# First loads in smaller pieces, P1 and P2 in two PSUM banks, and the last product in three banks of a factorization-machine kernel

## The chip, the cores and the metric

The kernel runs on one core of a Trainium2 chip. The metric is the device time of one execution in microseconds (us), median of a few runs. A profile of one execution is shown beside it.

## The reference

All data is float32. `x` is 1024 x 512 (batch, feature), `weight` is 64 x 512 x 512 (embedding, feature, model), `lin_w` is 512 x 512, `lin_b` has 512 values.

```python
out_lin = x @ lin_w.T + lin_b
xv = jnp.einsum('bf,efm->bem', x, weight)
zp = jnp.einsum('bf,efm->bem', jnp.square(x), jnp.square(weight))
interaction = 0.5 * jnp.sum(jnp.square(xv) - zp, axis=1)
return out_lin + interaction
```

There are three parts: a linear layer, a large product `xv` whose squares are summed over the 64 embeddings, and `zp`, which after the sum over embeddings is one product of the squared `x` with the summed squares of the weights.

## The kernel before, in words

**Work and tiling.** Features are split as 128 partitions times four slices k. Every matrix product is cut into 2 x 2 blocks and done by a scheme of seven block products (P1 to P7) with sums of blocks ahead of them and behind them; for `xv` the scheme is applied twice, one inside the other. Three stretches follow each other on TensorE:

- the linear layer: seven products of blocks of `x` (A11, A12, A21, A22 and sums R3, R5, R6, R7 of them) and blocks of `lin_w` (and sums lt1 to lt4 of them). It is written through `lin_product`, which calls `big_product` (L397);
- `xv`: eight groups of seven trees with seven products each (`tree`, L558, matmuls at L580), the bulk of the time;
- `zp`: seven products again (`zp_product`, L768, also through `big_product`), whose results are added to the output with the linear part.

A `big_product` fills a PSUM tile of two banks, [128, 2, 512]: half u = 0 or 1 holds two batch tiles of 128 rows with 256 model columns each. One half is two batch tiles times two slices k, four matmuls in the code and, in the records, eight weight loads and eight matmul instructions of 128x256 (each float32 matmul shows as two). With `by_k=True` the product is cut into four steps (k, u), so that it can start on the first slices.

**First loads.** `x` comes in transposed (`xT`, feature by batch). SP's queue brings eight pieces of 256 KB into `oa0` to `oa3`, ScalarE's queue four pieces of 256 KB of `lin_w` into `ob0` and `ob1` (L323 to L331). A11 is `oa0` (x slices k = 0 and 1, first batch half), A12 is `oa1` (k = 2 and 3), A21 and A22 are `oa2` and `oa3`, the second batch half. `lin_w`'s blocks are `ob0` (k = 0, 1) and `ob1` (k = 2, 3), each with column halves c = 0 and 1. Rows of a transfer are 2 KB. After these, SP's queue brings the weights.

**Zero matmuls.** VectorE zeroes the tile `t4_1`, and TensorE multiplies it by itself twice, 512 columns wide, into the bank pair `b2_1`, which is later overwritten (L334 to L338).

**P1, P2 and what follows.** P1 = A11 x block (0,0) of `lin_w` goes to `b2_0`. ScalarE copies each half of P1 to `b2_1`, where P6 and P7 are added to it later. P2 = A12 x block (1,0) is accumulated on P1 in `b2_0`, and a ScalarE copy takes the sum to `ob2`, which is stored. P4 = A22 x lt4 goes to `b1`, P5 = R5 x lt1 to `b3`, and so on (L458 to L478). VectorE makes lt1 to lt4 in `column_sums` (L385): t1 = b[1] - b[0], t2 = b[3] - t1, t3 = b[3] - b[1], t4 = b[2] - t2. The products need these; R5 = A22 - A21 and the other sums come from `x_sum` (L357). ScalarE copies A11, A12 and A22 into `x_all` (L355).

**The end.** The last product, `zp` P4, goes to `b2_1`; `add_part` (L749) subtracts half of it from the output rows in `w22a`, in two halves of 512 columns per partition on VectorE, and each half is stored by a transfer of 256 KB.

**What sets the order.** `Plan` (L30) is a list scheduler that runs when the program is built. Each step has a cost on its engine, reads, writes, and, for TensorE, a key that fixes its place. `order` gives each engine its fixed sequence; a VectorE, ScalarE, GpSimd or SP step is taken by the latest time at which it may start. `landing` tells the planner when a load is expected. Semaphores between engines are added to the emitted order automatically, from the tiles that are read and written. So a planned time decides only the order; the chip decides when.

Of the kernel before, what the change touches and what calls it, by code (L numbers as in the profile page):

```python
# [12 lines left out]
AF = mybir.ActivationFunctionType  # L13
ALU = mybir.AluOpType
AX = mybir.AxisListType

P = 128
G = 2
# [8 lines left out]
PE, DVE, ACT, POOL, SP = "PE", "DVE", "ACT", "POOL", "SP"  # L27
# [156 lines left out]
def kernel(  # L184
# [34 lines left out]
    nc = tc.nc  # L219
    NG, NQ, _, NCB, KH, N = weight.shape  # L220
    B = xT.shape[1]
    M = out.shape[1]
    NB = B // P
# [4 lines left out]
    H = B // 2  # L228
    Q = B // 4
# [11 lines left out]
    buf = {}  # L241
# [35 lines left out]
    plan = Plan()  # L277
# [18 lines left out]
    def act(o, i, func, reads, writes, cost=1.04):  # L296
        def emit(_):
            if func is None:
                nc.scalar.copy(o, i)  # L299
            else:  # L300
                nc.scalar.activation(o, i, func)  # L301

        plan.add({ACT: cost}, emit, reads, writes)
# [10 lines left out]
    def dma(o, i, reads, writes, move=1.75):  # L314
        plan.add({SP: 0.45}, lambda _: nc.sync.dma_start(o, i), reads, writes, land=2.0, move=move)


    x_src = xT.rearrange("(p k) b -> p k b", k=NK)
    lw_src = lin_wT.rearrange("(p k) m -> p k m", k=NK)
    def landing(name, at):  # L320
        plan.add({SP: 0.0}, None, (), (name,), land=at)

    for h, order in enumerate(((0, 1, 2, 3), (2, 3, 0, 1))):  # L323
        for at, k in enumerate(order):
            q, r = divmod(k, KH)
            n, l = f"oa{2 * h + q}", f"ob{q}"
            nc.sync.dma_start(buf[n][:, r, :], x_src[:, k, ts(h, H)])
            landing((n, r), (4.4 + 1.6 * at, 10.2 + 0.9 * at)[h])
            if h == 0:
                nc.scalar.dma_start(buf[l][:, r, :], lw_src[:, k, :])  # L330
                landing((l, r), 4.4 + 1.6 * at)  # L331


    zero = buf["t4_1"]  # L334
    nc.vector.memset(zero, 0.0)  # L335
    for j in range(G):
        nc.tensor.matmul(buf["b2_1"][:, j, :], zero[:, 0:P], zero, start=True, stop=True)  # L337
    plan.add({PE: 4.0}, None, (), (("b2_1", 0), ("b2_1", 1)), key=-2000)  # L338

    def block4(i):  # L340
        return buf[f"X{i}"][:, 0:4, :].rearrange("p (k q) b -> p k (q b)", k=2)
# [2 lines left out]
    a_buf = {"A11": "oa0", "A12": "oa1", "A21": "oa2", "A22": "oa3"}  # L344

    def a_parts(*names):
        return tuple((a_buf[n], r) for n in names if n in a_buf for r in range(KH)) + tuple(
            n for n in names if n not in a_buf
        )

    def a_ap(n):
        return buf[a_buf[n]] if n in a_buf else block4(int(n[1]))

    for i, n in ((1, "A11"), (2, "A12"), (4, "A22")):
        act(block4(i), a_ap(n), None, a_parts(n), (f"R{i}",))  # L355
# [23 lines left out]
    HM = M // 2  # L379

    def quarter(ap):

        return ap.rearrange("p a (b m) -> p (a b) m", b=2)
# [13 lines left out]
    def big_product(bank, lhs, rhs, first, keys, by_k=False):  # L397

        (a, a_names), (b, b_names) = lhs, rhs
        steps = [(u, [k]) for k in range(KH) for u in range(G)]  # L400
        for (u, ks), key in zip(steps if by_k else [(u, range(KH)) for u in range(G)], keys):
            def emit(_, u=u, ks=ks):
                for j in range(2):
                    for k in ks:
                        nc.tensor.matmul(  # L405
                            buf[bank][:, u, ts(j, HM)],
                            a[:, k, ts(2 * u + j, P)],
                            b[:, k, :],
                            start=first and j == 0 and k == 0,
                            stop=k == KH - 1,  # L410
                            skip_group_check=True,
                        )

            names = sum((a_names[k:k + 1] + b_names[k:k + 1] for k in ks), ()) if by_k else (
                a_names + b_names
            )
            plan.add({PE: PAIR * len(ks) / KH}, emit, names + ((bank, u),), ((bank, u),), key=key)

    def both_halves(bank):
        return (bank, 0), (bank, 1)  # L420

    lw_quad = [buf[f"ob{q}"][:, :, ts(c, HM)] for q in range(2) for c in range(2)]
    lw_names = [tuple((f"ob{q}", r) for r in range(KH)) for q in range(2) for _ in range(2)]
    lt = {
        k: buf[("p5_2", "p53_2")[(k - 1) // 2]][:, (k - 1) % 2, :].rearrange(
            "p (k m) -> p k m", k=KH
# [1 line left out]
        for k in range(1, 5)  # L428
    }
    lt_names = {k: (("lt", k),) for k in range(1, 5)}  # L430
    column_sums(DVE, lw_quad, lt, lw_names, lt_names)
    lhs = {i: (a_ap(n), a_parts(n)) for i, n in (
        (1, "A11"), (2, "A12"), (4, "A22"), (5, "R5"), (6, "R6"), (7, "R7"), (3, "R3"))}
    rhs = {1: (lw_quad[0], lw_names[0]), 2: (lw_quad[2], lw_names[2]),
           3: (lw_quad[3], lw_names[3]), 4: (lt[4], lt_names[4]),
           5: (lt[1], lt_names[1]), 6: (lt[2], lt_names[2]), 7: (lt[3], lt_names[3])}

    def lin_product(p, bank, first, key, last=None, by_k=False):
        keys = [key, last or key + 0.2, key + 0.4, key + 0.6]
        big_product(bank, lhs[p], rhs[p], first, keys, by_k)  # L440

    def lin_store(n, h, c):
        dma(lin_dram[:, ts(h, NB // 2), ts(c, HM)], quarter(buf[n]), (n,), (("lind", h, c),))

    def lin_last(n, bank, sign):

        def emit(_):
            if sign > 0:
                nc.vector.tensor_add(buf[n], buf[bank], buf[n])
            else:  # L450
                nc.vector.scalar_tensor_tensor(
                    buf[n], buf[n], -1.0, buf[bank], ALU.mult, ALU.subtract
                )

        reads = both_halves(bank) if bank.startswith("b") else (bank,)
        plan.add({DVE: 1.14}, emit, (n, *reads), (n,))

    lin_product(1, "b2_0", True, -1000, by_k=True)  # L458
    for u in range(G):
        act(buf["b2_1"][:, u, :], buf["b2_0"][:, u, :], None, (("b2_0", u),), (("b2_1", u),), 0.56)  # L460
    lin_product(2, "b2_0", False, -999, by_k=True)
    act(buf["ob2"], buf["b2_0"], None, both_halves("b2_0"), ("ob2",))
    lin_store("ob2", 0, 0)
    lin_product(4, "b1", True, -998)
    act(buf["c_0"], buf["b1"], None, both_halves("b1"), ("c_0",))
    lin_product(5, "b3", True, -997)
    act(buf["c_1"], buf["b3"], None, both_halves("b3"), ("c_1",))
    lin_product(6, "b2_1", False, -996)
# [11 lines left out]
    for lo, hi in ((0, 1), (1, 7)):  # L480
        a11, a21, a12, a22, s1, s2, s4 = (x_all[:, lo:hi, s, :] for s in range(7))
        raw, names, done = (tuple(f"{c}{i + 1}" for i in range(lo, hi)) for c in "RXY")
# [8 lines left out]
    def used(*names):  # L491

        plan.add({SP: 0.0}, None, (), names, land=-plan.HOP)

    for n in tuple(a_buf.values()) + ("ob0", "ob1"):
        used(n, (n, 0), (n, 1))
    for b in ("b1", "b3", "b2_0", "b2_1"):
        used(b, *both_halves(b))
    used("p5_2", ("lt", 1), ("lt", 2))
# [157 lines left out]
    for g in range(NG):  # L657
# [6 lines left out]
        order = ORDER if g else ORDER_0  # L664
# [12 lines left out]
        if g + 1 < NG:  # L677
            names = tuple((acc_name[g], *k) for k in acc_parts)
# [18 lines left out]
    for h, c in blocks:  # L697
        n, rows = lin_all[h, c], ts(h, NB // 2)
# [10 lines left out]
    lhs = {p: (buf[xe[b]], (xe[b],)) for p, b in ((1, (0, 0)), (2, (0, 1)), (4, (1, 1)))}  # L709
    a21 = (buf[xe[1, 0]], (xe[1, 0],))  # L710
    for p, a, b, kind in (
# [6 lines left out]
        a, b = (lhs[z] if isinstance(z, int) else z for z in (a, b))  # L718
# [5 lines left out]
        for q in range(2) for c in range(2)  # L724
# [5 lines left out]
    rhs = {1: (w2_quad[0], w2_names[0]), 2: (w2_quad[2], w2_names[2]),  # L730
           3: (w2_quad[3], w2_names[3])}
# [13 lines left out]
    out_dst = out.rearrange("(n p) m -> p n m", p=P)  # L745
    last_key = 7 * (7 * NG - 1) + PLACE[4]
    bank_a, bank_2, bank_b, bank_3 = "b1", "b2_0", "b2_1", "b3"

    def add_part(h, c, bank, store, halves=False):  # L749

        n = lin_all[h, c]
        for u in range(G) if halves else (slice(None),):
            o, b = buf[n][:, u], buf[bank][:, u]
            name = (n, u) if halves else n
            plan.add(
                {DVE: 0.61 if halves else 1.14},
                lambda _, o=o, b=b: nc.vector.scalar_tensor_tensor(  # L757
                    o, b, -0.5, o, ALU.mult, ALU.add
                ),
                (((bank, u),) if halves else both_halves(bank)) + (n,), (name,),  # L760
            )
            if store:
                lo = NB // 2 * h + (2 * u if halves else 0)
                src = o.rearrange("p (b m) -> p b m", b=2) if halves else quarter(o)
                dma(out_dst[:, lo:lo + (2 if halves else 4), ts(c, HM)], src, (name,), (),
                    0.9 if halves else 1.75)

    def zp_product(p, bank, first, key):  # L768
        big_product(bank, lhs[p], rhs[p], first, [last_key + key, last_key + key + 0.2])
# [14 lines left out]
    zp_product(3, bank_3, False, 5)  # L784
    add_edge(0)
    add_part(0, 1, bank_3, True)
    zp_product(4, bank_b, True, 6)
    add_part(1, 0, bank_b, True, True)

    for op, engine in plan.order():  # L790
        if op.emit:
# [32 lines left out]
```

## Time and profile before

| | us |
|---|---|
| median of 3 runs | 1409.09 (1408.12 to 1409.17) |
| profiled execution | 1408.17 |
| its span, first to last instruction | 1406.4 |
| TensorE busy | 1398.7 |
| GpSimd busy | 1039.1 |
| VectorE busy | 1079.7 |
| ScalarE busy | 693.4 |

The span is the time from the first to the last instruction of the core; the time of the execution is a little longer. In the profile, PE is TensorE's matmuls, PEld its weight loads, DVE VectorE, ACT ScalarE, POOL GpSimd, SP SyncE, whose queue starts most transfers; "q" marks the sequencer or the queue of an engine. L12 is line 12 of the kernel. Groups of instructions carry the tile written and the tiles read (out<-in, without buffer numbers: `b` stands for `b1`, `b3`, `b2_0` and `b2_1`, and `p` for the buffers that hold lt1 to lt4 at the start). The mean granted TensorE clock in the record is 0.999 of full speed.

### The profile page before, as it was taken

How to read it: one execution, taken by the hardware profiler on the slowest of the kernel's cores; microseconds unless marked ns; L12 is line 12 of the kernel's file. 1: busy time of each engine (PE TensorE's matmuls, PEld its weight loads, DVE VectorE, ACT ScalarE, POOL GpSimd, SP SyncE). 2: the span in 40 equal slices, each digit the busy share in tenths (PEclk: the TensorE clock that was granted, in tenths of full speed). 3: DMA queues.
4: the chain of work that ended last, by engine and by line, in shares of the span. 5: the costliest groups of instructions: out<-in, count | busy, mean ns of one | idle time of the engine just before them, and what ended most of it. 6: DMA issues, size and time to landing. Idle time of an engine off the chain costs nothing.

```text
span 1406.4 us, 10559 instructions
## 1 busy us (share of the span) xinstructions
PE 1398.7 (99%) x3364; PEld 639.1 (45%) x3364; DVE 1079.7 (77%) x929; ACT 693.4 (49%) x721; POOL 1039.1 (74%) x706
## 2 busy tenths in 40 slices
PE   9999999999999999999999999999999999999998
PEld 6444444444444444444444444444444444444446
DVE  7977696867959687696867859687696867859676
ACT  3545363544636455463544636455463545636442
POOL 5686786958678686776958678596777958678694
PEclk9999999999999999999999999999999999999999
DMA  5673562917538183562917537283563907447355
GB/s 224 164 174 96 124 179 80 237 46 178 155 97 206 45 222 96 134 175 85 232 39 185 148 105 198 55 224 85 144 182 81 228 31 194 138 113 194 90 119 118
DMA packets 53863, 197.57 MB, mean 140 GB/s; under 512 B 19120, under 2 KB 29360, under 8 KB 31920
## 3 DMA queue, kind: packets, MB, share of 16 engines
q0 software_dynamic: 15312, 84.81, 31.4%
q1 hardware_dynamic: 37920, 111.03, 22.4%
q10 hardware_dynamic: 576, 1.05, 0.2%
q8 instruction: 28, 0.46, 0.1%
q14 instruction: 27, 0.22, 0.0%
HBM read 173.93 MB, written 6.16 MB: 128 GB/s over the span
## 4 chain that ended last, share of the span: by engine, by line
PE 99%; DVE 0%; ACT 0%; DVEq 0%; issue 0%; ACTq 0%
PE b L580 96%; PE b L405 4%; PE b L337 0%; ACT b L299 0%; DVE w22a L757 0%; DVEq L820 0%; DVE t L335 0%; ACTq L299 0%
## 5 line engine op out<-in xcount | busy, mean ns | idle before, releaser
L580 PE MATMUL b<-t,x_all 128*128 128x512 f32 x1792 | 805.9, 592 | 0.0
L580 PEld LDWEIGHTS b<-t,x_all 128*128 128x128 f32 x1792 | 340.4, 190 | 427.8 <-issue 422.4
L580 PE MATMUL b<-w,x_all 128*128 128x512 f32 x768 | 358.1, 592 | 0.0
L287 POOL TENSOR_TENSOR t<-w 128x512 f32<-128x512 f32 x128 | 177.1, 1384 | 155.4 <-PE b L580 86.5
L299 ACT COPY p<-b 128x1024 f32<-128x1024 f32 x161 | 161.9, 1006 | 165.4 <-PE b L580 165.4
L580 PEld LDWEIGHTS b<-w,x_all 128*128 128x128 f32 x768 | 145.9, 190 | 183.3 <-issue 172.9
L287 POOL TENSOR_TENSOR t<-w,t 128x512 f32<-128x512 f32 x128 | 177.1, 1384 | 62.7 <-PE b L580 62.7
L301 ACT ACTIVATE oa<-oa 128x1024 f32<-128x1024 f32 x124 | 129.7, 1057 | 139.0 <-DVE oa L287 136.1
L580 PE MATMUL b<-T,x_all 128*128 128x512 f32 x384 | 180.4, 592 | 0.0
L308 DVE TENSOR_REDUCE acc<-oa 128x16 f32<-128x1024 f32 x124 | 149.0, 1211 | 38.7 <-ACT oa L301 38.7
L299 ACT COPY b<-b 128x1024 f32<-128x1024 f32 (+1 forms) x116 | 114.2, 985 | 125.1 <-PE b L580 120.8
L308 DVE TENSOR_REDUCE w_sum<-wsq 128x16 f32<-128x1024 f32 x128 | 154.7, 1210 | 19.4 <-ACT wsq L301 19.4
L287 DVE TENSOR_TENSOR oa<-b,p 128x1024 f32<-128x1024 f32 x95 | 115.9, 1220 | 41.0 <-PE b L580 40.8
L287 POOL TENSOR_TENSOR t<-T 128x512 f32<-128x512 f32 x64 | 90.3, 1411 | 57.8 <-issue 33.2
L301 ACT ACTIVATE wsq<-w 128x1024 f32<-128x1024 f32 x96 | 97.9, 1056 | 66.0 <-DVE w_sum L308 66.0
L301 ACT ACTIVATE c<-c 128x1024 f32<-128x1024 f32 x68 | 70.1, 1056 | 92.4 <-POOL c L287 63.0
L580 PEld LDWEIGHTS b<-T,x_all 128*128 128x128 f32 x384 | 73.0, 190 | 91.8 <-issue 91.4
L287 DVE TENSOR_TENSOR ob<-b,p 128x1024 f32<-128x1024 f32 x48 | 58.6, 1221 | 67.3 <-PE b L580 67.3
L287 DVE TENSOR_TENSOR p<-b,p 128x1024 f32<-128x1024 f32 x79 | 96.3, 1219 | 17.5 <-PE b L580 17.4
L287 POOL TENSOR_TENSOR t<-T,t 128x512 f32<-128x512 f32 x64 | 81.3, 1270 | 20.5 <-PE b L580 20.5
L287 POOL TENSOR_TENSOR ob<-ob,p 128x1024 f32<-128x1024 f32 x32 | 91.9, 2884 | 0.0
L287 POOL TENSOR_TENSOR c<-oa,p 128x1024 f32<-128x1024 f32 x32 | 90.7, 2834 | 0.0
(86 smaller groups left out, 1408.6 us busy)
## 6 DMA issues: line engine op xcount, KB each, us to landing
w<-weight SPq DMA_DIRECT2D x48, 1024.0 KB, 4.9
T<-weight POOLq DMA_DIRECT2D x45, 1024.0 KB, 8.5
T<-weight SPq DMA_DIRECT2D x30, 1024.0 KB, 7.0
w<-weight POOLq DMA_DIRECT2D x16, 1024.0 KB, 11.2
w<-T POOLq DMA_DIRECT2D x16, 1024.0 KB, 6.9
w22a<-weight SPq DMA_DIRECT2D x8, 1024.0 KB, 8.1
w22b<-weight SPq DMA_DIRECT2D x8, 1024.0 KB, 8.1
oa<-xT SPq DMA_DIRECT2D x8, 256.0 KB, 6.5
```

Of the source, the lines that this page charges most:

```text
L287: f(o, a, b)
L299: nc.scalar.copy(o, i)
L301: nc.scalar.activation(o, i, func)
L308: lambda _: nc.vector.tensor_reduce(o, i.rearrange("p a (m e) -> p a m e", e=E), axis=AX.X, op=ALU.add),
L405: nc.tensor.matmul(buf[bank][:, u, ts(j, HM)], a[:, k, ts(2 * u + j, P)], b[:, k, :], start=first and j == 0 and k == 0, stop=k == KH - 1, ...
L580: nc.tensor.matmul(buf[b][:, j, :], buf[f"X{i}"][:, SLOT[p], ts(j, P)], op, start=first, stop=True, skip_group_check=True,)
```

## The change

1. The first loads: the x slice k = 0 comes in two pieces of 256 batch columns; the lin_w pieces are halves by columns, first the left half (k = 0, k = 1, then k = 2 and 3 in one), then the right half (k = 0 and 1, then k = 2 and 3). Their rows are 1 KB. In all there are nine x transfers and five of lin_w. The names that the planner tracks become (tile, slice, part), so that step (k, u) of P1 waits for its own pieces.
2. `nc.scalar.preload_act_table(AF.Square)` stands after the loads of ScalarE's queue.
3. The zero matmuls read a constant instead of a zeroed tile; they are one of 512 columns and one of 256, into `b2_0`.
4. P1 goes to `b2_1` and stays there; P2 goes to `b1` on its own. ScalarE copies P1 to `ob2`, and VectorE adds P2 (`lin_last`). P4 goes to `b2_0`.
5. The last product is done in three pieces of 2, 1 and 1 batch tiles in `b1`, `b2_1` and `b2_0`, and each piece is added and stored on its own.

```diff
-    for h, order in enumerate(((0, 1, 2, 3), (2, 3, 0, 1))):
-        for at, k in enumerate(order):
-            q, r = divmod(k, KH)
-            n, l = f"oa{2 * h + q}", f"ob{q}"
-            nc.sync.dma_start(buf[n][:, r, :], x_src[:, k, ts(h, H)])
-            landing((n, r), (4.4 + 1.6 * at, 10.2 + 0.9 * at)[h])
-            if h == 0:
-                nc.scalar.dma_start(buf[l][:, r, :], lw_src[:, k, :])
-                landing((l, r), 4.4 + 1.6 * at)
-    zero = buf["t4_1"]
-    nc.vector.memset(zero, 0.0)
-    for j in range(G):
-        nc.tensor.matmul(buf["b2_1"][:, j, :], zero[:, 0:P], zero, start=True, stop=True)
-    plan.add({PE: 4.0}, None, (), (("b2_1", 0), ("b2_1", 1)), key=-2000)
+    def load_x(h, k, lo, hi, at):
+        n, r = f"oa{2 * h + k // KH}", k % KH
+        nc.sync.dma_start(buf[n][:, r, lo * Q:hi * Q], x_src[:, k, h * H + lo * Q:h * H + hi * Q])
+        for u in range(lo, hi):
+            landing((n, r, u), at)
+    def load_lw(ks, c, at):
+        l, r = f"ob{ks[0] // KH}", ks[0] % KH
+        nc.scalar.dma_start(
+            buf[l][:, r:r + len(ks), ts(c, N // 2)],
+            lw_src[:, ks[0]:ks[0] + len(ks), ts(c, N // 2)],
+        )
+        for k in ks:
+            landing((l, k % KH, c), at)
+    load_x(0, 0, 0, 1, 4.2)
+    load_lw([0], 0, 4.2)
+    load_x(0, 0, 1, 2, 4.7)
+    load_lw([1], 0, 5.2)
+    load_x(0, 1, 0, 2, 5.6)
+    load_lw([2, 3], 0, 6.6)
+    load_x(0, 2, 0, 2, 7.0)
+    load_lw([0, 1], 1, 7.8)
+    load_x(0, 3, 0, 2, 8.0)
+    load_lw([2, 3], 1, 9.0)
+    for at, k in enumerate((2, 3, 0, 1)):
+        load_x(1, k, 0, 2, 9.6 + 0.9 * at)
+    nc.scalar.preload_act_table(AF.Square)
+    zero = nc.const_aps.tensor(0.0, [P, N])
+    for width in (N, N // 2):
+        nc.tensor.matmul(
+            buf["b2_0"][:, 0, 0:width], zero[:, 0:P], zero[:, 0:width], start=True, stop=True
+        )
+    plan.add({PE: 3.0}, None, (), (("b2_0", 0), ("b2_0", 1)), key=-2000)
...
-            names = sum((a_names[k:k + 1] + b_names[k:k + 1] for k in ks), ()) if by_k else (
-                a_names + b_names
-            )
+            names = a_names + b_names
+            if by_k:
+                names = sum((a_names[2 * k + u:2 * k + u + 1] + b_names[k:k + 1] for k in ks), ())
...
-    lin_product(1, "b2_0", True, -1000, by_k=True)
-    for u in range(G):
-        act(buf["b2_1"][:, u, :], buf["b2_0"][:, u, :], None, (("b2_0", u),), (("b2_1", u),), 0.56)
-    lin_product(2, "b2_0", False, -999, by_k=True)
-    act(buf["ob2"], buf["b2_0"], None, both_halves("b2_0"), ("ob2",))
+    lin_product(1, "b2_1", True, -1000, by_k=True)
+    act(buf["ob2"], buf["b2_1"], None, both_halves("b2_1"), ("ob2",))
+    lin_product(2, "b1", True, -999, by_k=True)
+    lin_last("ob2", "b1", 1)
     lin_store("ob2", 0, 0)
-    lin_product(4, "b1", True, -998)
-    act(buf["c_0"], buf["b1"], None, both_halves("b1"), ("c_0",))
+    lin_product(4, "b2_0", True, -998)
+    act(buf["c_0"], buf["b2_0"], None, both_halves("b2_0"), ("c_0",))
...
-    def add_part(h, c, bank, store, halves=False):
+    def add_part(h, c, bank, store, piece=None):
...
+        tiles = piece or (0, 4)
+        o = quarter(buf[n])[:, tiles[0]:tiles[1], :]
+        b = quarter(buf[bank])[:, 0:tiles[1] - tiles[0], :]
...
-    zp_product(4, bank_b, True, 6)
-    add_part(1, 0, bank_b, True, True)
+    for at, (bank, piece) in enumerate(
+        ((bank_a, (0, 2)), (bank_b, (2, 3)), (bank_2, (3, 4)))
+    ):
+        def emit(_, bank=bank, piece=piece):
+            for j in range(*piece):
+                for k in range(KH):
+                    nc.tensor.matmul(
+                        quarter(buf[bank])[:, j - piece[0], :], lhs[4][0][:, k, ts(j, P)],
+                        rhs[4][0][:, k, :], start=j == piece[0] and k == 0, stop=k == KH - 1,
+                        skip_group_check=True,
+                    )
...
+        add_part(1, 0, bank, True, piece)
```

More of the change, by code (lines that the diff above doesn't have):

```diff
@@ L346, in a_parts @@
     def a_parts(*names):
-        return tuple((a_buf[n], r) for n in names if n in a_buf for r in range(KH)) + tuple(
-            n for n in names if n not in a_buf
-        )
+        return tuple(
+            (a_buf[n], r, u) for n in names if n in a_buf for r in range(KH) for u in range(2)
+        ) + tuple(n for n in names if n not in a_buf)
     def a_ap(n):
@@ L412, in emit @@
                         )
-            names = sum((a_names[k:k + 1] + b_names[k:k + 1] for k in ks), ()) if by_k else (
-                a_names + b_names
-            )
+            names = a_names + b_names
+            if by_k:
+                names = sum((a_names[2 * k + u:2 * k + u + 1] + b_names[k:k + 1] for k in ks), ())
             plan.add({PE: PAIR * len(ks) / KH}, emit, names + ((bank, u),), ((bank, u),), key=key)
@@ L422 @@
     lw_quad = [buf[f"ob{q}"][:, :, ts(c, HM)] for q in range(2) for c in range(2)]
-    lw_names = [tuple((f"ob{q}", r) for r in range(KH)) for q in range(2) for _ in range(2)]
+    lw_names = [tuple((f"ob{q}", r, c) for r in range(KH)) for q in range(2) for c in range(2)]
     lt = {
@@ L495 @@
     for n in tuple(a_buf.values()) + ("ob0", "ob1"):
-        used(n, (n, 0), (n, 1))
+        used(n, *((n, r, u) for r in range(KH) for u in range(2)))
     for b in ("b1", "b3", "b2_0", "b2_1"):
@@ L747 @@
     bank_a, bank_2, bank_b, bank_3 = "b1", "b2_0", "b2_1", "b3"
-    def add_part(h, c, bank, store, halves=False):
+    def add_part(h, c, bank, store, piece=None):
         n = lin_all[h, c]
[L752 to L766, printed above, removed]
+        tiles = piece or (0, 4)
+        o = quarter(buf[n])[:, tiles[0]:tiles[1], :]
+        b = quarter(buf[bank])[:, 0:tiles[1] - tiles[0], :]
+        name = (n, piece) if piece else n
+        plan.add(
+            {DVE: 0.08 + 0.265 * (tiles[1] - tiles[0])},
+            lambda _: nc.vector.scalar_tensor_tensor(o, b, -0.5, o, ALU.mult, ALU.add),
+            (((bank, 0),) if piece else both_halves(bank)) + (n,), (name,),
+        )
+        if store:
+            lo = NB // 2 * h
+            dma(out_dst[:, lo + tiles[0]:lo + tiles[1], ts(c, HM)], o, (name,), (),
+                0.45 * (tiles[1] - tiles[0]))
     def zp_product(p, bank, first, key):
@@ L786 @@
     add_part(0, 1, bank_3, True)
-    zp_product(4, bank_b, True, 6)
-    add_part(1, 0, bank_b, True, True)
+    for at, (bank, piece) in enumerate(
[8 more added lines that the diff above has]
+                        skip_group_check=True,
+                    )
+        plan.add({PE: 0.86 * (piece[1] - piece[0])}, emit,
+                 lhs[4][1] + rhs[4][1] + both_halves(bank), both_halves(bank),
+                 key=last_key + 6 + 0.2 * at)
+        add_part(1, 0, bank, True, piece)
     for op, engine in plan.order():
```

## The prediction

> **What bounds the kernel now.** I read the shares of busy time, then PE's waits, then the chain of waits at the front, then both ends in the timeline.
>
> ```profile
> PE 1398.7 (99%) x3364; PEld 639.1 (45%) x3364; DVE 1079.7 (77%) x929; ACT 693.4 (49%) x721; POOL 1039.1 (74%) x706
> ```
>
> ```profile
> PE b L337 <- DVE t L335: 1.5, 1, 1.5
> PE b L405 <- ACT b L299: 1.4, 2, 0.7
> ```
>
> TensorE bounds it. PE's only waits in 1406 us are these three (engine and line that waited, releaser: us, times, longest), all in the first 12 us; beyond them there is only the stretch after its last matmul. So the change can win only before PE's stream closes up, and after it ends. The chain of waits, 0 to 40 us (start, us, what):
>
> ```profile
> 0.92 0.50 DVE t L335
> ...
> 1.46 3.58 PE b L337 x4
> 5.05 3.65 PE b L405 x16
> ...
> 8.72 0.58 ACT b L299
> ...
> 9.35 1.14 PE b L405 x4
> ...
> 10.57 0.58 ACT b L299
> ...
> 11.19 18.40 PE b L405 x84
> ```
>
> Zero matmuls run from 1.46 to 5.05, P1 (16 instructions) to 8.70, then P2 is cut twice by ScalarE's copies of P1 (8.70 to 9.35, 10.49 to 11.19). From 11.19 PE never waits. The timeline shows when the next product, P4, has its operand lt4 (start, us, engine):
>
> ```profile
> 10.13 0.69 DVE L287 TENSOR_TENSOR p<-ob,p 128x512 f32<-128x512 f32 x1 [0.28 <-DMA ob<-lin_wT]
> 10.74 0.69 DVE L287 TENSOR_TENSOR p<-ob,ob 128x512 f32<-128x512 f32 x1
> 11.34 0.68 DVE L287 TENSOR_TENSOR p<-ob,p 128x512 f32<-128x512 f32 x1
> 13.89 3.62 PE L405 MATMUL b<-p,oa 128*128 128x256 f32 x16
> ```
>
> The three DVE lines are t2, t3 and t4 (lt4); t2 starts when the last lin_w load lands. So lt4 is ready at 12.02 and P4 starts at 13.89: **1.87 us of slack**, all that the front can give before the loads bind. The issues by line agree: with the SP issue starts 0.75, 1.21, 1.68, 2.16, 4.69, 5.06, 5.83, 6.32 the eight x loads land at about 4.85, 6.1, 9.2, 10.3, 11.0, 11.7, 12.2, 12.9; A22, P4's other operand, is the fifth and sixth (11.7). The tail:
>
> ```profile
> 1397.93 3.62 PE L405 MATMUL b<-x_all,w 128*128 128x256 f32 x16
> ...
> 1401.59 1.29 DVE L757 SCALAR_TENSOR_TENSOR w22a<-b,w22a 128x512 f32<-128x512 f32 x2 [2.23 <-PE b L405]
> 1402.31 0.97 SPq L315 DMA_DIRECT2D out<-w22a  x2
> ```
>
> Both DVE halves stand after PE's end at 1401.57, though the first half's eight matmuls are over near 1399.75: a reader of one half of a PSUM tile waits for the last write to the tile. The same shows at 10.57: the copy of P1's second half waited for P2's first step, which writes the other half.
>
> **What the Trainium skill says.**
> - "TensorE: Matmul & The Clock Gate", part 1, What's actually happening: the array runs at half clock until it has been busy for a window of about 3.4 us; the window runs freely. The trace agrees: the zero matmuls take 0.86 to 1.22 us, half rate, the first of P1 483 ns, then 215 ns from start to start; full rate came about 3.7 us after 1.46.
> - "DMA: Bandwidth & Descriptors", Queues, rings and completion order: each DMA engine alternates between queues after a whole packet of several descriptors. In the trace the ScalarE and SP queues move about equal counts of equal 2 KB rows until 8 us (488 and 468), which does not tell bytes from rows.
> - The same page, Anatomy of one DMA: a fixed cost near 2 us. The last two stores took 2.3 us at the median.
> - "ScalarE: Activation LUTs", What ACT_TABLE_LOAD costs: 1283 ns. The trace has 1.28 us at 6.13.
>
> **The change part by part.**
>
> *Zero matmuls on a constant.* The 0.48 us memset goes. PE starts with the other engines, 0.75 to 0.95, instead of at 1.46. The work is 1.5 products for 2: 3.58 x 0.75 = 2.7 us, ending about 3.55. Its end was 5.05 just as the first load had landed (4.97), so it no longer stands before P1; it leaves PE idle until P1 (third rival).
>
> *Loads divided.* Bytes are unchanged: 3.1 MB. Rows of lin_w and of the first x slice become 1 KB. The trace prices a row by queue share: 2 KB rows at 8 to 10 us cost 76 ns of an engine; 1 KB rows of lin_b, at 1350 to 1355, 53 ns. lin_w goes from 512 x 76 to 1024 x 53 ns, over 16 engines +0.96 us; the x slice +0.24. So what ends at the last lin_w piece lands up to 1.2 us later; if 1 KB rows cost just half, 38 ns, 0. The first pieces are half as large. The first 256 rows took from 2.0 to 4.0 us; half the bytes need half of that, or all of it if the start is limited by rows. P1 then starts at 4.1 to 5.0; I take 4.4. The queues: at most eight transfers were in flight (SP's fifth x load waited 2.1 us, until the first lin_w load had landed), so with 14 transfers x slice 3 and the last lin_w piece wait for the first landing near 4.2, on SP and on ScalarE's queue. Behind the latter stands only the table load, then the copy of A11, which started its table load at 6.13 anyhow. Four x loads and the weight loads stand behind SP's wait, but the earlier transfers are still moving then, so I count 0; uncovered it is the 2.1 us that SP waited before.
>
> *P1 and P2 in two banks.* Both copies between banks (1.16 us of ACT) and both PE gaps, 0.65 + 0.70 = 1.35 us, go. P1 and P2 are 32 instructions of 0.215 us = 6.9 us: from 4.4, with the start cold until about 5.2, to 11.7 at the earliest. A DVE add, about 1.22 us by the x1024 rows that read PSUM, comes in. DVE has gaps of 0.69 us before 13.05 and work due 10 us later (the X sums for the second tree), and the bank b1 is needed again near 33 us, so it costs 0; uncovered, at most 1.2. What is late next is P4: it needs the last lin_w piece plus t2, t3, t4 (2.02 us from the landing) and A22. Before, that landing was at 10.0; I take +1.1 for 1 KB rows, 11.1, so lt4 at 13.2 and A22 at 12.8. P4 starts at 13.25: **front gain 0.65 us**. Bounds: 13.89 - 11.7 = +2.2 if loads do not bind; -1.6 if the last piece is starved (second rival). P5 then starts 3.45 later, at 16.7; its R5 (13.05 to 14.28 before, 1.1 later) is there at 15.4, also with the added DVE op in front. Later loads have slack: the first tree matmul is at 29.4, its first weights at 15.5.
>
> *Table load earlier.* 1.28 us off an idle ScalarE; the copy it preceded feeds X sums that nothing here waits for: 0.
>
> *Last product in three banks.* The same 16 matmuls, 3.62 us. The first piece (8 matmuls) is read at about 1399.8, the second at 1400.7, both under PE. After PE's end one 128x256 DVE op remains, 0.42 us by the 128x256 adds at the front, instead of 1.29: -0.87. Its store is 128 KB instead of 256; the two stores moved 0.53 MB at about 340 GB/s, so -0.38 on the last landing. SP's two earlier stores are issued (0.37 to 0.39 us each) before 1401.6. Banks b1 and b2_0 were last read by 1397.03, so nothing waits. **Tail gain 1.25 us** (0.9 to 1.4: the store's fixed part might hide the smaller size).
>
> Sum: 0.65 + 1.25 = 1.9. The profiled execution took 1408.17 us, its span 1406.4 and 1.77 around it: 1406.27. The runs' median, 1409.09, is 0.92 above it. Two of three runs lie there; if that is a clock released later in P1, the new slack under the loads covers most of it, so I add a third, 0.3: **1406.6 us**.
>
> **The rivals.**
> 1. *The loads do not bind.* From 5 to 7 us the engines moved 200 to 260 GB/s where they had 400 before and after (PE, PEld, DVE, ACT, POOL, clock, DMA share, GB/s):
>
> ```profile
> 5.50:6.00 0.50, 0.50 (x4) 0.44 (x3) 0.09 (x1) 0.00 (x0) 0.00 (x0) 1.00 0.56 197
> 8.00:8.50 0.50, 0.50 (x4) 0.26 (x2) 0.00 (x0) 0.47 (x1) 0.00 (x0) 1.00 1.09 418
> ```
>
> Some 0.9 MB should have come where 0.5 did, and the second to third slice took 3.1 us instead of 1.2. The page names no cause; if dividing the loads removes it, landings come up to 1.8 us earlier, and P4 starts at 11.9: gain 2.0 + 1.25, 1404.9, with the 0.3, 1405.2. Against: more rows, not fewer.
> 2. *Queues alternate by row.* Then 1 KB rows of lin_w get half of the bytes of x: the last piece comes after 16 rounds of 106 and 48 of 129 ns, 7.9 us instead of 64 x 76 = 4.9, so at 13.0 to 13.4, and P4 at 15.1 to 15.5. Loss 1.6, tail 1.25: 1408.5, with the 0.3, 1408.8. For: equal row counts. Against: the skill's whole packets.
> 3. *The clock is not released (slower).* The zero matmuls ran 3.58 us straight into P1; now 2.7, then an idle gap near 0.9. If a window with such a gap doesn't count, P1 and P2 run at 0.43 us an instruction. Each us of it costs 0.5. A release at 8.2 is still hidden by P4's operands; from 12.0 on (P4 at 15.1) the loss exceeds the tail's gain, and this decides. At 15.4, three windows after 5.2, 25 instructions are done from 4.4 and 7 follow: P4 at 16.9, loss 3.0, net 1.75: 1409.9, with the 0.3, 1410.2. Against: PE would be busy three quarters of the time.
> 4. *The tail doesn't split:* DVE still waits for all three pieces. Then 0.69 + 0.42 + 0.42 follow PE: +0.24 of DVE, -0.38 of store, with the front 0.79 in all: 1407.4, with the 0.3, 1407.7.
>
> **How the numbers follow.** Forecast 0.50 (own range 1405.8 to 1407.6), rivals 0.25, 0.13, 0.08, 0.04. A measurement can tell about 0.2%, 2.8 us: below 1406.3 is faster, above 1411.9 slower. Faster: the first rival and a third of the forecast, 0.25 + 0.17 = 0.42. Slower: the far end of the third rival, 0.03. Same: 0.55. The range, 1404.7 to 1408.9, takes in the forecast and most of rivals 1, 2 and 4; the clock case and the edges stay out.
>
> **What would show it.** Right: zero matmuls from under 1 us to about 3.6; no ACT copy into a bank; P2 following P1 with, at most, waits for DMA; P4 at 13.0 to 13.5, released by DVE's t4; one 128x256 DVE op after PE's end, then one 128 KB store. Rival 1: P4 before 12.3. Rival 2: t2 starting after 12.5. Rival 3: P1's instructions at 0.43 us after 6 us. Wrong altogether: a wait on PE after 17 us.

## The result and the profile after

The changed kernel takes 1406.16 us (median of 16 runs, 1405.46 to 1407.15), the kernel before 1408.93 (16 runs, 1408.12 to 1409.60). The ratio is 0.9980, with a 95% interval of 0.9973 to 0.9988: 2.8 us less. The profiled execution took 1406.02 us, its span is 1404.3, against 1408.17 and 1406.4.

PE's waits after (line waited, releaser: us, times, longest):

```profile
PE b L358 <- PEq L848: 0.8, 1, 0.8
PE b L428 <- DVE p L287: 0.5, 1, 0.5
```

The wait for the zeroed tile is only the common start now, both waits for ScalarE's copies are gone, and a new one of 0.5 us for VectorE has come in: it is P4 waiting for t4. The timeline of the front:

```profile
3.48 8.68 PE L428 MATMUL b<-ob,oa 128*128 128x256 f32 x32
...
10.98 0.69 DVE L287 TENSOR_TENSOR p<-ob,p 128x512 f32<-128x512 f32 x1 [0.58 <-DMA ob<-lin_wT]
...
11.59 0.42 DVE L287 TENSOR_TENSOR x_all<-x_all 128x256 f32<-128x256 f32 x1
11.93 0.69 DVE L287 TENSOR_TENSOR p<-ob,p 128x512 f32<-128x512 f32 x1
12.53 0.68 DVE L287 TENSOR_TENSOR p<-ob,ob 128x512 f32<-128x512 f32 x1
12.67 3.50 PE L428 MATMUL b<-p,oa 128*128 128x256 f32 x15 [0.51 <-DVE p L287]
```

P1 and P2 are one unbroken run of 32 instructions. t2 starts at 10.98, when the last lin_w piece has landed (10.89), a sum of blocks of `x` follows, then t4 and only then t3 (the row with `ob,ob`); before, t3 came first. P4 starts at 12.67 where it started at 13.89: 1.22 us at the front. From there to the end of PE's last matmul both kernels take the same time within 0.1 us (1387.57 after, 1387.66 before). The tail:

```profile
1396.62 3.62 PE L814 MATMUL b<-x_all,w 128*128 128x256 f32 x16
...
1398.55 0.69 DVE L780 SCALAR_TENSOR_TENSOR w22a<-b,w22a 128x512 f32<-128x512 f32 x1 [0.50 <-PE b L814]
1399.27 1.81 SPq L315 DMA_DIRECT2D out<-w22a  x3
1399.42 0.42 DVE L780 SCALAR_TENSOR_TENSOR w22a<-b,w22a 128x256 f32<-128x256 f32 x1 [0.17 <-PE b L814]
1400.28 0.42 DVE L780 SCALAR_TENSOR_TENSOR w22a<-b,w22a 128x256 f32<-128x256 f32 x1 [0.44 <-PE b L814]
```

Two of the three pieces are read while PE works; after PE's end at 1400.24 one VectorE operation of 0.42 us is left. From PE's end to the span's end it is 4.01 us, before 4.86: 0.85 at the tail. Together 1.22 + 0.85 + 0.09 = 2.16 us, the difference of the spans (1406.41 and 1404.25). The medians differ by 2.8 because the execution of before that was profiled was a quick one, 0.76 us under its median, and that of after only 0.14.

The last store, issued at 1400.73, lands at 1402.54, yet the span ends 1.71 us later, where before it ended 1.05 after the last landing (1405.36). SP's closing instructions behind the landing show why (line, queue, kind, count: ns min/median/max, first and last start), first after:

```profile
L855 SPq EVENT_SEMAPHORE  x3: 28/28/28, 1402.6 to 1402.8; - x3
...
L855 SPq EVENT_SEMAPHORE  x4: 28/28/28, 1403.1 to 1403.3; - x4
...
L855 SPq DRAIN  x2: 7/7/7, 1403.4 to 1403.5; - x2
```

then before:

```profile
L820 SPq EVENT_SEMAPHORE  x2: 28/28/28, 1405.4 to 1405.5; - x2
L820 SPq DRAIN  x2: 7/7/7, 1405.6 to 1405.6; - x2
```

A transfer tells of its landing through a semaphore, a counter that SP can wait for. At the end SP waits for the eight transfer semaphores one after another. The seven waits behind the landing had all long been met; six of them start 0.06 to 0.09 us after the one ahead, and one 0.36 us after it (1402.77 to 1403.13), for a cause that stays open. The semaphores are dealt to the SP and ScalarE transfers in turn, and the waits go from number 0 to 7. In the changed kernel the last store holds number 0, so seven waits come after its landing; before it held number 5, with two behind it.

### The profile page after: what moved, and what is told of

Its sections match the earlier page's. It is cut to its first block, busy times and chain, and to the rows that moved or that the text cites. A ratio compares the mean times of both kernels' runs of the same rounds, so it can differ in the third digit from the quotient of the medians.

```text
span 1404.3 us, 10555 instructions
## 1 busy us (share of the span) xinstructions
PE 1399.0 (100%) x3364; PEld 640.3 (46%) x3364; DVE 1081.1 (77%) x930; ACT 692.1 (49%) x719; POOL 1040.2 (74%) x706
## 3 DMA queue, kind: packets, MB, share of 16 engines
q10 hardware_dynamic: 1104, 1.05, 0.2%
## 4 chain that ended last, share of the span: by engine, by line
PE 99%; DMA 1%; DVE 0%; ACTq 0%; issue 0%
PE b L602 96%; PE b L428 3%; DMA ob<-lin_wT 0%; DMA oa<-xT 0%; PE b L814 0%; ACTq L333 0%; DVE p L287 0%; DVE w22a L780 0%; DVE x_all L287 0%
## 6 DMA issues: line engine op xcount, KB each, us to landing
w<-weight POOLq DMA_DIRECT2D x16, 1024.0 KB, 11.2
```

## The experiments

The theory after reading this: the front's gain comes from P1 and P2 in two banks, with P4's operands as the new bound; the tail's from the three banks, less what the closing waits take back. The rivals: the divided loads carry the front's gain; the end has another cause; and the clock, which in the changed kernel rose only near 6.6 us (the spacing of the matmuls goes from 0.43 to 0.215 us there), matters more than the profile shows. Ratios below are to the kernel before as it ran beside each of them (1408.77 or 1408.78 us; it was 1408.93 beside the changed kernel).

**The front alone.** The changed kernel with the old last product.

```diff
-    for at, (bank, piece) in enumerate(
-        ((bank_a, (0, 2)), (bank_b, (2, 3)), (bank_2, (3, 4)))
-    ):
...
+    zp_product(4, bank_b, True, 6)
+    add_part(1, 0, bank_b, True, True)
```

> The changed front with the old last product (two halves of one PSUM tile, two stores of 256 KB). If front and tail are independent, the front alone moves P4's start from 13.89 to 12.67 us and the time from 1408.9 to 1407.7 (1.2 less). Rival, that most of the gain comes from the tail: 1408.5. The last store takes the eighth transfer semaphore in turn (number 7), so SP's closing waits should end within 0.2 us of its landing.

1407.33 us, ratio 0.9989 (0.9982 to 0.9995): 1.45 us less. P4 at 12.96. SP's last wait came 0.01 us after the landing, as expected, and 0.91 us followed the landing instead of before's 1.05. All the same the end, 4.91 us from PE's last matmul, was no shorter than before's 4.86: this time the last store took 2.65 us from issue to landing, and 2.46 in before's execution.

**The tail alone.** The kernel before with the last product in three banks.

```diff
-    zp_product(4, bank_b, True, 6)
-    add_part(1, 0, bank_b, True, True)
+    for at, (bank, piece) in enumerate(
+        ((bank_a, (0, 2)), (bank_b, (2, 3)), (bank_2, (3, 4)))
+    ):
...
```

> The front of before with the last product in three banks. In the profile of the changed kernel the last store landed 2.3 us after PE's end instead of 3.8, but SP then still went through seven semaphores of older transfers, about 0.1 us each. Here the last store takes number 6 of 8, with one wait behind it. Theory of the closing waits: the tail alone gives 1.5 us, 1407.4. Rival, that the tail's gain is 0.8 as the changed kernel's span shows and its end has another cause: 1408.1.

1407.51 us, ratio 0.9990 (0.9981 to 0.9998): 1.27 us less. The interval, 0.3 to 2.7 us, takes in the theory's 1.5 and the rival's 0.8; the trace decides. From PE's end to the span's end it is 3.33 us, 1.53 less than before, as the theory has it. In its profiled execution P1 ended, and all after it came, 0.7 us later than in before's (zero matmuls 3.78 us instead of 3.58, P1 4.14 instead of 3.65), so the front, unchanged in the program, moves by that much from one execution to another. Front and tail add up within their intervals, 0.11% and 0.10% against 0.20%, though the tail here is spared some 0.7 us of closing waits that the changed kernel has.

**One transfer less.** The changed kernel with A21 loaded at once.

```diff
-    for at, k in enumerate((2, 3, 0, 1)):
+    for at, k in enumerate((2, 3)):
         load_x(1, k, 0, 2, 9.6 + 0.9 * at)
+    nc.sync.dma_start(buf["oa2"], x_src[:, 0:KH, ts(1, H)])
...
```

> The changed kernel with the two x loads of A21 in one transfer of 512 KB: one transfer less, so the last store takes number 7 of the eight semaphores instead of number 0, and SP's closing waits stand ahead of its landing. Nothing else should move: P4 at 12.7. Theory of the closing waits: 0.7 us less than the changed kernel, 1405.4. Rival, that the end has another cause: 1406.1, no change.

1405.69 us, ratio 0.9976 (0.9967 to 0.9986), 0.5 less than the changed kernel's median. The time alone does not settle it, since P4 was not at 12.7 but at 11.94 in its profiled execution: the last lin_w piece had landed 0.7 us earlier (10.16, not 10.89). The stretch after PE's end does:

| last store's semaphore | kernels | us from its landing to the span's end | us from PE's end to the span's end |
|---|---|---|---|
| 0 | changed; without zero matmuls | 1.71, 1.71 | 4.01, 4.00 |
| 6 | tail alone; whole loads; bridged | 1.04, 0.98, 0.98 | 3.33, 3.26, 3.25 |
| 7 | one transfer less; bridged with one more | 0.92, 0.92 | 3.21, 3.20 |

All have the three pieces. Against number 7, with no wait behind the landing, seven waits cost 0.79 us and one 0.06 to 0.12.

**Whole loads.** The changed kernel with the first loads as before.

```diff
-    load_x(0, 0, 0, 1, 4.2)
-    load_lw([0], 0, 4.2)
...
+    for k in range(NK):
+        load_x(0, k, 0, 2, 4.4 + 1.6 * k)
+        l, r = f"ob{k // KH}", k % KH
+        nc.scalar.dma_start(buf[l][:, r, :], lw_src[:, k, :])
...
```

> The changed kernel with the first loads undivided, as before (eight of x, four of lin_w, 256 KB each, 2 KB rows). Theory: P4 is set by t4 behind the last lin_w load and by P2 behind the last x slice, which undivided land at 10.0 and 10.3; P1 starts at 5.0 instead of 3.5, P2 ends near 12.6, t4 near 12.0, so P4 starts at 12.5 to 12.8, as in the changed kernel: 1405.6 to 1406.1 (the last store takes number 6, so the end is 0.6 us shorter). Rival, that dividing the loads is what gains at the front: P4 at 13.5 or later, 1406.6 or more.

The median of 14 runs is 1407.82, ratio 0.9988 (0.9980 to 0.9995), but it stands for two groups: three runs lie at 1404.7 to 1405.1, ten at 1407.6 to 1408.3, one between. The profile fell on the lowest. P4 started at 12.18, and the lower group is even under what was expected. The upper group fits the rival's numbers, so the time leaves open whether the loads set it. One more execution of the same program:

> The same program as e4_whole_loads, one more look, for a profile of an upper run (about 7 in 10). Clock theory: P1's instructions 0.43 us apart until 8 us or later, and P4 near 15. Load theory: 0.215 us apart, with waits for transfers. If it is a lower run, it shows P4 near 12.1 again and tells nothing new.

It took 1407.28, between the groups; by its timeline it is an upper run. The timelines of P1 and P2, first of the lower, then of the upper run:

```profile
5.14 7.20 PE L424 MATMUL b<-ob,oa 128*128 128x256 f32 x32 [1.45 <-DMA ob<-lin_wT]
```

```profile
5.18 9.40 PE L424 MATMUL b<-ob,oa 128*128 128x256 f32 x32 [1.50 <-DMA ob<-lin_wT]
```

The same 32 instructions take 2.2 us longer, with no wait between them in either run. The stretch view counts them (us, PE busy and instructions, granted clock, share of DMA, GB/s):

```profile
7.00:8.00 1.00, 1.00 (x6) 1.00 1.03 393
```

```profile
7.00:8.00 1.00, 1.00 (x4) 1.00 1.00 348
```

In the upper run they stand 0.43 us apart until about 9.8 us, half rate. The column of the granted clock reads 1.00 in both, but it takes 1.00 wherever the trace has no record of the clock: that record begins, at full rate, at 3.95 us in the lower run and at 9.73 in the upper. So the clock theory holds here.

**The bridge.** Whole loads, and zero matmuls long enough to reach P1.

```diff
-    for width in (N, N // 2):
+    for width in (N, N, N // 2):
```

> Undivided loads as in e4_whole_loads, but zero matmuls of 512, 512 and 256 columns, which run at half clock from 0.8 to about 5.1 us and so up to P1's first load. e4_whole_loads had runs near 1404.9 and runs near 1407.9. Theory: the upper runs are those in which the idle 1.5 us of PE before P1 cost a clock window, so that P1 and P2 ran at half clock for 3.4 us or more longer. Then all runs here lie near 1404.9 (1404.5 to 1405.5). Rival, that the loads land late in the upper runs: the two groups stay, median 1407 or more.

1405.24 us, ratio 0.9975 (0.9964 to 0.9985), all eight runs between 1404.93 and 1405.73: one group, the lower one. The chain of waits has nothing but PE from the start:

```profile
0.78 4.60 PE b L354 x6
5.39 22.76 PE b L424 x104
```

P4 starts at 12.44, without a wait. The idle 1.5 us ahead of P1 was what cost the upper runs 3 us. By the ratios this version lies some 0.7 us under the changed kernel; the end alone is 0.76 shorter (3.25 against 4.01 us, semaphore 6 against 0), so the front is about as good as with divided loads.

**No zero matmuls.** The changed kernel without them.

```diff
-    zero = nc.const_aps.tensor(0.0, [P, N])
-    for width in (N, N // 2):
-        nc.tensor.matmul(
-            buf["b2_0"][:, 0, 0:width], zero[:, 0:P], zero[:, 0:width], start=True, stop=True
-        )
```

> The changed kernel without any zero matmuls. P1 starts at 3.5 us as before. Theory: in the changed kernel the zero matmuls bought little, since the clock rose only at 6.9 us and P4 waits for t4 until 12.7 anyway; a rise at 6.9 costs nothing here, one a window later, at 10.3, puts P4 at 13.8, 1.1 later: 1406.2 to 1407.3, median 1406.7. Rival, that without them the rise comes two windows later or more: 1408 or more.

1406.27 us, ratio 0.9982 (0.9974 to 0.9990), like the changed kernel. P1 and P2 took 8.74 us from 3.49, against 8.68 from 3.48: the clock rose at nearly the same time (its record begins at 6.69 us, and at 6.57 in the changed kernel), and P4, at 12.59, waited for t4 again. In the changed kernel the 1.5 zero matmuls buy nothing.

**The divided loads alone,** on the kernel before: zero matmuls, P1, P2 and the last product are left as they were.

```diff
+    load_x(0, 0, 0, 1, 4.2)
+    load_lw([0], 0, 4.2)
...
-    lw_names = [tuple((f"ob{q}", r) for r in range(KH)) for q in range(2) for _ in range(2)]
+    lw_names = [tuple((f"ob{q}", r, c) for r in range(KH)) for q in range(2) for c in range(2)]
```

> The kernel before with only the division of the first loads; zero matmuls on the zeroed tile, P1 and P2 in one bank with the two copies, no earlier table load, and the old last product. Theory: the division alone gives almost nothing, since the zero matmuls end at 5.05 as before, the two stalls of 1.35 us stay, and the last lin_w piece lands later: P4 between 13.4 and 14.2, 1408.3 to 1409.1 (of which 0.2 less is due to the place of the last store among the transfer semaphores). Rival, that dividing the loads carries the front's gain: 1407.5 or less.

1408.73 us, ratio 1.0002 (0.9993 to 1.0010): nothing. P4 started at 14.26, just past the expected 14.2, and PE's waits are those of before:

```profile
PE b L357 <- DVE t L355: 1.5, 1, 1.5
PE b L425 <- ACT b L299: 1.4, 2, 0.7
```

**Two pieces instead of three** in the last product.

```diff
-        ((bank_a, (0, 2)), (bank_b, (2, 3)), (bank_2, (3, 4)))
+        ((bank_a, (0, 2)), (bank_b, (2, 4)))
```

> The changed kernel with the last product in two pieces of two batch tiles, each in its own tile (b1 and b2_1), two stores of 256 KB; the last store takes semaphore number 7. From PE's end to the span's end: e3_lane, with three pieces and the same number 7, has 3.17 us. Two pieces leave a VectorE operation of 0.69 instead of 0.42, +0.27, and a store of 256 KB instead of 128. If the smaller store saves what its bytes need, 0.38, the stretch is 3.8; if the store's fixed part hides its size, 3.45.

A single execution, 1405.32 us. From PE's end (1399.57) to the span's end it is 3.98 us, against 3.21 with three pieces and the same semaphore: 0.77 more. Of this 0.27 is VectorE's and 0.50 the store's, which took 2.30 us from issue to landing instead of 1.80. So the smaller store saves all that its bytes were priced at, 0.38, and a little more.

**The version that the runs point to:** the bridge with the first x slice in two halves, one transfer more.

> The version that the experiments point to: e5_bridge (undivided loads but for the first x slice, zero matmuls up to P1, P1 and P2 in two banks, last product in three) with one transfer more, the first x slice in two halves, so that the last store takes semaphore number 7. 0.1 us less than e5_bridge at the end, P4 at 12.1 to 12.5: 1405.1 (1404.8 to 1405.5), faster than both kernels. Rival, that the 1 KB rows of the first slice delay the others: 1405.5 or more.

1405.34 us, ratio 0.9976 (0.9966 to 0.9985), as the bridge alone; one of the ten runs lies apart, at 1406.85. The end was 0.05 us shorter (3.20), which the time cannot tell. P4 started at 12.68, later than expected: P1 started at 5.18 and ran at half rate until about 6.4. Both versions are faster than the kernel before. By the ratios they lie 0.6 to 0.7 us under the changed kernel; their intervals and its own (0.9973 to 0.9988) overlap, and what carries the difference is the shorter end that the traces show.

## Why the prediction was right, and where its terms were off

The prediction was 1406.6 us, the measurement 1406.16, and the two mechanisms are those it named: P1 and P2 without the stalls until P4's operands bind, and two thirds of the last product's reading moved under PE. By its own steps:

- *Zero matmuls* from 0.75 to 0.95 until 3.55: they ran from 0.78 to 3.68. They delay nothing, and they help nothing (no zero matmuls, 1406.27).
- *P1 starts at 4.4, at the earliest 4.1:* it started at 3.48, outside the bounds. The first pieces landed 2.5 to 2.7 us after their issue, with 381 GB/s moving at 3.0 to 3.5 us; the price for rows at the start, taken from the slow first 256 rows of before, did not hold for 1 KB rows. It made no difference, as P4 did not wait for P1. (Of before's first load the prediction says 4.97 in one place and 4.85 in another; the trace has 4.86.)
- *Last lin_w piece at 11.1:* it landed at 10.89. Over the six executions with divided loads it varied, 10.2 to 11.2, and with it P4's start in the five that have two banks, 11.9 to 13.0.
- *lt4 2.02 us after it:* 1.64, counted from t2's start at 10.98. This term of the sum was mis-sized: I kept the order t2, t3, t4 of the old profile, and in the changed program the planner puts t4 ahead of t3. It does so with whole loads too, and not with the divided loads alone, so the loads are not its cause; which of the other parts is, no run shows. That is 0.4 of the 0.57 us by which the front's 0.65 fell short of 1.22. Another 0.1 is t2's start, and the rest is rounding in the sum: 11.1 and 2.02 make 13.12, where the prediction has 13.2 and then 13.25.
- *Divided loads:* alone they give nothing, and the front is as good without them, if the zero matmuls reach P1: P4 at 12.18 and 12.44 with whole loads and the clock up, 12.68 with the first x slice alone in two, against 11.94 to 12.96 with divided ones. So the front's gain is that of the two banks, by elimination: no run has them alone, but with whole loads P1 starts no earlier (5.14 to 5.29 us) than before (5.00), and the table load concerns ScalarE only. From P1's start to P4's it is 8.89 us before and 7.04 in the lower run of the whole loads, so the two stalls had cost 1.85 us, more than their 1.35 us of idle time. The +1.1 us for the last piece was right in kind and somewhat large: it landed at 10.7 us in the mean of those six executions and at 9.9 in the five with whole loads. It costs little here, since with whole loads P4 waited for P2 instead.
- *VectorE's added sum* stood at 13.13, beside work that was not waited for: 0, as said.
- *Tail 1.25:* 0.85. VectorE's 0.87 was right: the last store is issued 0.49 us after PE's end instead of 1.35. The store's 0.38 was too small: it landed 1.81 us after its issue instead of 2.46, 0.65 less. What the sum left out is the stretch behind the last landing. The prediction let the span end with the landing; the change moved the last store from semaphore 5 to 0, and five more closing waits took 0.66 us back (1.71 against 1.05).
- *The 0.3 us for the spread of before, a third of it covered:* not shown. The profiled execution lay 0.76 us under the median before and 0.14 after, but that is one execution of each, and the 16 runs spread no less after (1405.46 to 1407.15) than before (1408.12 to 1409.60). What the traces do show is the part that the clock has: in the old front its record begins at 4.72, 5.85 and 6.24 us (before, divided loads alone, tail alone) and P4 starts at 13.89, 14.26 and 14.56; in the changed kernel it begins at 6.57, and P4 at 12.67 waits for t4 alone.
- *The sum:* the front gave 0.57 more than foretold and the tail 0.40 less. That the whole came within 0.4 us owes something to luck, as these two nearly cancel.

Of the rivals, the starved queue did not come (t2 before 12.5). The tail did split. The clock was late, as the third rival feared, at 6.57 us, but within the 8.2 us that it named as hidden. The same mechanism cost 3 us in most runs with whole loads, where the gap was 1.5 us and P2 itself set P4's start. Whether the dip of the loads from 5 to 7 us comes from the order of the transfers stays open: it was there in the changed kernel (199 GB/s at 5.5 to 6.0), and weaker with the same divided loads but no zero matmuls (266) and with whole loads (266 and 311), which are the loads of before (197). So it varies with something else, and no run was made for it.

"TensorE: Matmul & The Clock Gate" has, in part 1, What's actually happening, a window of about 3.4 us that runs freely. The runs agree: the record of full rate in the traces is 1396.05 us long in some executions and 1399.46 in others, 3.41 apart, and it begins at a different time in each, 4.72 (before), 6.57 (changed), 6.69 (without zero matmuls), 3.95 and 9.73 us (whole loads, lower and upper run). The traces also tell how full a window must be; eleven of the twelve have the record. Counted back 3.41 us from its beginning, TensorE was busy for 85% of the last window in the lower run and for 94% or more in the others. Of the windows ahead of these, after which the clock did not rise, the fullest is one of 70% in the changed kernel; in the upper run of the whole loads two were busy for 62% and 56%. So 2.9 us of zero matmuls filled a window only where the window happened to lie around them; where it cut through them, the idle 1.5 us kept the next one from being full too. This fits the two groups. That the limit lies between 70 and 85% rests on these few executions.

## What to carry to other kernels

When a stall is taken off the busiest engine, look up how long before its old start the next step's other operands were ready: that slack (1.87 us here) bounds the gain, however long the stall is, and the operand's own chain on the other engines is to be read in the new order, not the old one. Dividing loads brings time only if the first use is what the path waits for; here its one merit was to leave no idle gap ahead of the first product, and longer zero matmuls did that as well. A change at the very end should be read to the span's end, through the closing waits, and not to the last landing.

## What the hardware showed that was not expected

- The record of the granted clock begins only with the rise to full rate, and the views read 1.00 ahead of it, while 128x256 matmuls stand 0.43 us apart, half rate. At the start the spacing tells the clock, the column does not.
- In these traces the clock rose after a window of 3.41 us in which TensorE was busy for 85% or more, and not after one busy for 70%.
- One program can fall into two groups of times 3 us apart for an idle gap of 1.5 us ahead of its first real matmuls.
- Waits on semaphores that have long been met still cost SP time: seven of them behind the last store cost 0.79 us, over a quarter of what the whole change gains.
